# Scores of gathered rows and the chain of maxima moved to earlier hops in the first two layers of a graph attention kernel

## The chip, the cores and the metric

The kernel runs on one core of a Trainium2 chip. The metric is the device time of one execution in microseconds (us). Before the change, three runs gave 7299.5, 7305.31 and 7309.96 us; the median is 7305.31 us.

## The reference, cut to what matters

The input is a graph with 6250 nodes of 256 features and 200,000 edges (`src`, `dst`), ordered by destination. Three graph attention layers run one after the other, the first two with four heads, the third with one; beside them stand a linear attention block and a mixture of eight experts. One attention layer computes:

```python
xh = (h @ W).reshape(n, heads, d)
a_s = (xh * att_src).sum(-1)
a_d = (xh * att_dst).sum(-1)
alpha = leaky_relu(a_s[src] + a_d[dst], 0.2)
amax = segment_max(alpha, dst)
e = exp(alpha - amax[dst])
z = segment_sum(e, dst)
out = segment_sum(xh[src] * (e / z[dst])[:, :, None], dst)
```

Every node has an edge to itself as well. So for each edge a row of its source node is fetched, a score is made, the largest score of the edges with one destination is found, and the rows are summed with the weights `exp(score - largest)`.

## The kernel before, in words

**Tiles.** The edges are cut into rows of 128, and 32 such rows make one round. Each layer has 51 rounds, written out one after the other in `sum_messages`. A gather (line 549) is one indirect DMA that GpSimd issues; it fetches the feature rows of 128 edges. Eight gathers fill one row group `g` of 8 x 128 edges, and a round has four row groups, 0 to 3. The pool of row groups has 8 buffers in the first layer, 9 in the second and 7 in the third (`nrows`).

**Rounds and hops.** A round is written as 16 hops (`for i in range(HSU)`). In hop i of round s, TensorE multiplies the one-hot matrices of two edge rows with their weighted gathered rows (`pair`, line 752), and VectorE adds the product of an earlier pair to the accumulator of the destination block (`add_up`, line 765). After the pairs of hops 3, 7, 11 and 15 a row group is free, and the next gathers into that buffer are issued (`gather`). With 8 buffers, the group that is issued in hop 4j + 3 of round s is group j of round s + 2. With 9 buffers, group j of round s + 2 is issued one freeing earlier, in hop 4j - 1.

**What is made for the next round.** While round s is summed, the weights of round n = s + 1 are made:

- `row_scores` (line 610): ScalarE copies the source scores out of a gathered row group into `asc`, one group at a time. It needs the gather landed. Before the change this is in hops 2, 4, 5 and 7.
- `spread` (line 603): TensorE brings the destination scores to the edges, in hops 0 to 8; VectorE sums three parts of them into `exs` in hop 11 (line 796).
- `scores` (lines 587 and 591): in every second round, TensorE makes the destination scores of two rounds in hops 1 to 4, and ScalarE copies them out in hop 5.
- `maxima`: a chain of ten links that finds the largest score of each destination. Link 0 is a TensorE transpose of `asc` (line 621); link 1 two VectorE scans and two products (625 to 630); link 2 TensorE (633); link 3 VectorE (637 to 646); link 4 TensorE and one VectorE product (649, 652); link 5 VectorE (655 to 670); link 6 TensorE (674 to 677); link 7 VectorE (681 to 694); link 8 the exponentials on ScalarE (696, 697); link 9 VectorE writes the weights and factors (701, 705).
- `weigh_step` (lines 715 and 722): VectorE and ScalarE multiply gathered rows with the weights, about two hops ahead of the pair that reads them.

A link is either early in its hop (ahead of `weigh_step`, `add_up` and `pair`) or late (behind the pair, ahead of `spread`). Before the change:

| Link | 0 | 1 | 2 | 3 | 4 | 5 | 6 | 7 | 8 | 9 |
|---|---|---|---|---|---|---|---|---|---|---|
| Works on | PE | DVE | PE | DVE | PE, DVE | DVE | PE | DVE | ACT | DVE |
| Hop | 7 late | 8 late | 9 early | 10 early | 10 late | 11 late | 12 early | 13 early | 14 early | 14 late |

**What sets the order.** `Order.keep` pins each engine to the order of the text. An engine whose next instruction waits holds up all that is written behind it on that engine. Pieces of other work (linear attention in the first layer, the finished blocks of every layer, the experts in the third) are dealt out at the end of hops by `beside`. SyncE issues the loads of tables and lanes in text order too; GpSimd issues gathers only. The chain and `scores` share one PSUM bank, `sm`, of which there is one.

Of the kernel before, what the change touches and what calls it, by code (L numbers as in the profile page):

```python
# [7 lines left out]
F32 = mybir.dt.float32  # L8
# [7 lines left out]
P = 128  # L16
# [7 lines left out]
SU = 32  # L24
# [430 lines left out]
def leaky(nc, out, x):  # L455
    nc.vector.scalar_tensor_tensor(out, x, SLOPE, x, op0=OP.mult, op1=OP.max)
# [26 lines left out]
def sum_messages(tc, pools, consts, q, node_rows, adn, h, acc, beside, begin, slot, last,  # L483
# [9 lines left out]
    nc = tc.nc  # L493
    lp, tb, gp, hp, tp, wk, pmp, smp = pools
# [46 lines left out]
    def gather(m):  # L541

        if m >= end * subs:
            return
        s, k = divmod(m, subs)
        t = rows[m] = gp.tile([P, SUB, W], F32, name="g")
        for c in range(SUB):
            i = k * SUB + c
            nc.gpsimd.indirect_dma_start(  # L549
                out=t[:, c, :], out_offset=None, in_=node_rows,  # L550
                in_offset=bass.IndirectOffsetOnAxis(ap=T[s]["src"][:, i:i + 1], axis=0))

    def load_lanes(m):

        if m >= end * subs:
            return
        t = lanes[m] = tp.tile([P, SUB, P], BF16, name="hot_t")
        load(tc, t, bass.AP(tensor=q["lane_rows"].tensor,
                            offset=q["lane_rows"].offset + m * SUB * P,
                            ap=[[0, P], [P, SUB], [1, P]]))  # L560

    def compare_lanes(m):
        if m < end * subs:
            nc.vector.tensor_scalar(lanes[m], lanes[m], consts["pidx"], None, op0=OP.is_equal)  # L564

    def hot(m):

        s, k = divmod(m, subs)
        if s >= end:
            return  # L570
        t = M[s].setdefault("hots", {})[k] = hp.tile([P, SUB, P], F32, name="hot")
        nc.vector.tensor_tensor(  # L572
            t, consts["lane_ps"][:, None, :].to_broadcast([P, SUB, P]),
            T[s]["lane"][:, k * SUB:(k + 1) * SUB, None].to_broadcast([P, SUB, P]),
            op=OP.is_equal)
# [5 lines left out]
    def scores(s):  # L581


        pt = bank()[:, :3 * hs].rearrange("p (k c) -> p k c", k=3 * h)
        for i in range(4):
            for k in range(i * 3 * h // 4, (i + 1) * 3 * h // 4):
                nc.tensor.matmul(pt[:, k, :], adt[:, k // 3, k % 3, :], T[s]["block_hot"],
                                 start=True, stop=True)
            yield
        A[s] = wk.tile([P, h, 3, SU], BF16, name="adc")  # L590
        nc.scalar.copy(A[s].rearrange("p k j c -> p (k j) c"), pt)
# [5 lines left out]
    def spread(s, c0, n):  # L597

        m = M[s]
        if c0 == 0:  # L600
            m["ex"] = smp.tile([P, SU, h, 3], F32, name="ex")
        for c in range(c0, c0 + n):
            nc.tensor.matmul(m["ex"][:, c], lanes[s * subs + c // SUB][:, c % SUB, :],  # L603
                             adc(s)[:, :, :, c // 2], start=True, stop=True)

    def row_scores(s, k):
        m = M[s]
        if k == 0:
            m["asc"] = wk.tile([P, h, SU], F32, name="asc")
        nc.scalar.copy(m["asc"][:, :, k * SUB:(k + 1) * SUB].rearrange("p h c -> p c h"),  # L610
                       rows[s * subs + k][:, :, body:])

    def maxima(s):

        m, t = M[s], T[s]
        asc = m["asc"]
# [34 lines left out]
        on = lp.tile([HEADS, HEADS], F32, name="on")  # L651
        nc.vector.tensor_scalar(on[:h, :h], consts["ident"][:h, :h], run, None, op0=OP.mult)
        yield
        u = lp.tile([P, 2, h, SU], F32, name="u")
        nc.vector.tensor_add(u[:, 0], asc, m["exs"])
        pick = lp.tile([P, 2, SU], F32, name="pick")
        nc.vector.tensor_tensor(pick[:hs], pc[:hs],
                                cmask[:, None, :].to_broadcast([hs, 2, SU]), op=OP.mult)
# [19 lines left out]
        mt = m["mt"] = sm[:, k:k + hs].rearrange("p (h c) -> p h c", h=h)  # L678
        yield

        nc.vector.tensor_tensor(u[:, 1], mt, m["exs"], op=OP.add)
        leaky(nc, u, u)
        w = m["w"] = wk.tile([P, h, SU], F32, name="w")
# [19 lines left out]
        for k in range(subs):  # L703
            i = slice(k * SUB, (k + 1) * SUB)
# [19 lines left out]
    def weigh_step(s, i):  # L724

        c = (i // 2 + 1) * GRP
        s, c = s + c // SU, c % SU
        if not 0 <= s < end:
            return
        if half:  # L730
            weigh(s, c + half + i % 2, 1, nc.scalar)
            if i % 2:
                weigh(s, c, half, nc.vector)
        else:
            weigh(s, c + i % 2 * 2, 2, nc.scalar)

    def blocks(s, k):
        if s >= end:
            return
        loads, M[s].setdefault("blocks", {})[k] = nc.values_load_multi_w_load_instructions(  # L740
            T[s]["block"][0:1, k * GRP:(k + 1) * GRP], engines=(mybir.EngineType.DVE,),
            min_val=0, max_val=NB - 1,
            skip_runtime_bounds_check_because="blocks are counted from 0 to NB - 1")

    sums = []

    def pair(s, i):
        m = M[s]
        t, k = rows[s * subs + 2 * i // SUB], 2 * i % SUB
        pm = pmp.tile([P, W], F32, name="pm")  # L750
        for j in range(2):
            nc.tensor.matmul(pm, m["hots"][2 * i // SUB][:, k + j, :], t[:, k + j, :],  # L752
                             start=(j == 0), stop=(j == 1))
        sums.append((s, i, pm))

    def add_up(ahead=1):
        while len(sums) > ahead:
            s, i, pm = sums.pop(0)
            b = bass.ds(M[s]["blocks"][i // GRP][i % GRP], 1)
            if i == 0:  # L760
                at = acc[:, b, :body].rearrange("p b (h d) -> p (b h) d", h=h)
                nc.vector.tensor_tensor(at, at, M[s]["fac"][:, :, None].to_broadcast([P, h, d1]),
                                        op=OP.mult)
            at = acc[:, b].rearrange("p b w -> p (b w)")
            nc.vector.tensor_tensor(at, at, pm, op=OP.add)  # L765
# [16 lines left out]
    for s in range(-1, end):  # L782
        n = s + 1
        made = n < end
        if made:
            M[n] = M.get(n, {})
        ahead = iter(())
        if n % 2 and n + 1 < end:
            ahead = scores(n + 1)
        for i in range(HSU):  # L790

            if made and i in (2, 4, 5, 7):
                row_scores(n, (2, 4, 5, 7).index(i))
            if made and i == 11:
                M[n]["exs"] = wk.tile([P, h, SU], F32, name="exs")
                nc.vector.tensor_reduce(M[n]["exs"].rearrange("p k c -> p c k"), M[n]["ex"],
                                        axis=AX.X, op=OP.add)
            if made and i in (9, 10, 12, 13, 14):
                next(chain)
            if s < 0 and i * GRP < NB:  # L800
                nc.vector.memset(acc[:, i * GRP:min(NB, (i + 1) * GRP), :], 0.0)

            weigh_step(s, i)
            add_up()
            if s >= 0:
                pair(s, i)
                if i % GRP == GRP - 1:
                    gather(s * subs + i // GRP + nrows)
            if i % GRP == 1 and (i > 1 or s >= 0):
                hot((n if i > 1 else s) * subs + (i // GRP - 1) % subs)  # L810
            if i % GRP == 2:
                k = i // GRP + 1
                blocks(s + k // subs, k % subs) if s >= 0 or k == subs else None
            if made and i == 7:
                chain = maxima(n)
            if made and i in (7, 8, 10, 11, 14):
                next(chain, None)

            if made and i < 9:
                spread(n, 4 * i - max(0, i - 5), 4 - i // 5)  # L820
                if i in (1, 3, 6, 8):
                    load_lanes(n * subs + (1, 3, 6, 8).index(i) + nlanes)
                if i in (1, 3, 5):
                    compare_lanes(n * subs + i // 2 + 1)
            if made and i == HSU - 1:
                compare_lanes((n + 1) * subs)
            if 1 <= i <= 5:
                next(ahead, None)
            if i == 8 and s + 3 not in T:
                tables(s + 3)  # L830
            if s >= 0:
                if s * HSU + i in slots:
                    slot(slots.index(s * HSU + i), lay)
                if i == HSU // 2 and s == end - 1:
                    last(lay)
                beside.step()
            order.keep()
        for x in (T, M):
            x.pop(s - 1, None)
# [520 lines left out]
class Experts:  # L1360
# [17 lines left out]
    def next(self):  # L1378
        while len(self.ready) < 3 and self.todo:
            self.more()  # L1380
        return self.ready[0]
# [302 lines left out]
```

## Time and profile before

| What | Value |
|---|---|
| Median of three runs | 7305.31 us |
| Profiled execution, its own time | 8248.33 us |
| Span in the profile (first to last instruction) | 8246.6 us |
| Mean granted TensorE clock | 0.797 |
| TensorE busy | 5848.3 us, 71% |
| VectorE busy | 4702.2 us, 57% |
| ScalarE busy | 3408.8 us, 41% |
| GpSimd busy | 4819.9 us, 58% |
| Gathers (line 549) | 4896, mean 979 ns |
| Transposes of `asc` (line 621) | 153, from 219.6 to 8080.6 us |

The profiled execution is 943 us longer than the median of the runs, so its parts cannot be taken over one to one. PE stands for TensorE, DVE for VectorE, ACT for ScalarE, POOL for GpSimd. A wait is written as: engine, tile and line that waited, an arrow, who ended the wait, and then the sum in us, the number of waits, and the longest. "Issue" means that the profile shows nothing it waited for, and "remote" that the semaphore that ended the wait could not be put down to an instruction. Ends of matmuls are modelled in this profile. The summing of the first layer lies between 271 and 2774 us, that of the second between 2906 and 5304, that of the third between 5409 and 8154.

### The profile page before, as it was taken

The page shows a single profiled execution, that of the slowest core. Times are in us where ns is not written, and L with a number is a line of the kernel's source. Part 1 is how long each engine was busy: PE and PEld are TensorE (multiplying, and loading weights), DVE is VectorE, ACT ScalarE, POOL GpSimd, SP SyncE. Part 2 cuts the span into 40 slices and gives each one's busy share as a digit, 9 for nine tenths or more (in the row PEclk, how much of TensorE's full clock was granted, in tenths as well). Part 3 has the DMA queues.
Part 4 walks back from the last instruction along what each step waited for, and adds up shares of the span by engine and source line. Part 5 has one row for each costly group of instructions (what it writes and reads, how often), then busy time and mean ns, then how long its engine had stood idle before and what let it go on. Part 6 is the DMA issues. An engine that isn't in the chain of part 4 may idle for free. (4 is left out here: it accounts for less than half of the span.)

```text
span 8246.6 us, 97731 instructions
## 1 busy us (share of the span) xinstructions
PE 5848.3 (71%) x24601; PEld 4071.4 (49%) x24601; DVE 4702.2 (57%) x13248; ACT 3408.8 (41%) x10628; POOL 4819.9 (58%) x4942
## 2 busy tenths in 40 slices
PE   4577777766666356555665666548888998988998
PEld 3355555544444244344444444336566666665666
DVE  4456676667765365555555665544555555555553
ACT  2345454444434234333333343324444444444443
POOL 2566566666666456666666666465555555655651
PEclk8787778776766677766667776769999999999999
DMA  5444444444444334444444444344555554554553
GB/s 162 118 128 130 118 134 123 127 126 135 140 125 121 94 109 130 120 123 122 122 124 130 124 125 129 94 113 143 143 146 144 149 146 143 157 144 135 151 148 96
DMA packets 616288, 1070.05 MB, mean 130 GB/s; under 512 B 193175, under 2 KB 348167, under 8 KB 615706
## 3 DMA queue, kind: packets, MB, share of 16 engines
q0 software_dynamic: 236672, 661.50, 29.1%
q1 hardware_dynamic: 370590, 389.03, 15.8%
q10 hardware_dynamic: 8444, 13.02, 0.4%
q8 instruction: 212, 3.47, 0.2%
q14 instruction: 370, 3.03, 0.1%
HBM read 1008.69 MB, written 56.03 MB: 129 GB/s over the span
## 5 line engine op out<-in xcount | busy, mean ns | idle before, releaser
L549 POOL DMA_INDIRECT g<-node_rows,src_t x4896 | 4791.2, 979 | 3165.2 <-issue 1332.1
L752 PE MATMUL pm<-g,hot 128*128 128x264 f32 (+1 forms) x9792 | 3345.2, 481 | 855.2 <-issue 392.4
L752 PEld LDWEIGHTS pm<-g,hot 128*128 128x128 f32 x9792 | 2156.1, 235 | 1542.6 <-issue 632.2
L722 ACT ACTIVATE g<-g,w 128x65 f32<-128x65 f32 (+1 forms) x8160 | 2378.0, 369 | 207.0 <-issue 203.0
L765 DVE TENSOR_TENSOR acc<-acc,pm 128x264 f32 (+1 forms) x2448 | 1030.6, 421 | 844.6 <-remote 327.1
L572 DVE TENSOR_TENSOR hot<-lane_ps,lane_t 128x1024 f32<-128x1024 f32 x612 | 743.6, 1215 | 0.0
L715 DVE TENSOR_TENSOR g<-g,lane_ps 128x520 f32<-128x520 f32 x816 | 558.9, 685 | 34.7 <-issue 31.7
L603 PEld LDWEIGHTS <-hot_t 128*128 128x128 bf16 x4896 | 357.1, 105 | 372.6 <-issue 171.0
L696 ACT ACTIVATE w<-w 128x128 f32<-128x128 f32 (+1 forms) x153 | 43.1, 282 | 1011.6 <-DVE w L684 686.9
L603 PE MATMUL ex<-adc,hot_t 128*128 128x12 bf16 (+1 forms) x4896 | 360.4, 179 | 87.5 <-issue 72.3
L1607 PE MATMUL fa<-moe_w,moe_h 128*128 128x256 f32 x1600 | 398.7, 392 | 30.4 <-DVE eo L1612 12.6
L1595 PE MATMUL fa<-et,moe_w 128*128 128x512 f32 (+1 forms) x832 | 396.1, 600 | 29.8 <-DVE eo L1612 13.2
L1595 PE MATMUL fk<-et,moe_w 128*128 128x512 f32 (+1 forms) x832 | 387.2, 588 | 11.9 <-DVE eo L1588 5.1
L1600 ACT ACTIVATE moe_h<-fa,moe_b 128x512 f32<-128x512 f32 (+1 forms) x208 | 137.6, 662 | 597.6 <-PE fa L1595 425.0
L1607 PE MATMUL fk<-moe_w,moe_h 128*128 128x256 f32 x1536 | 377.0, 389 | 8.0 <-DVE eo L1612 6.9
L610 ACT COPY asc<-g 128x32 f32<-128x32 f32 (+1 forms) x612 | 136.5, 223 | 528.9 <-DMA g<-node_rows,src_t 464.6
L1612 DVE SCALAR_TENSOR_TENSOR eo<-fa,share,eo 128x256 f32<-128x256 f32 x200 | 96.1, 480 | 432.7 <-PE fa L1607 212.2
L1607 PEld LDWEIGHTS fa<-moe_w,moe_h 128*128 128x128 f32 x1600 | 297.9, 193 | 83.0 <-ACT moe_h L1600 18.2
L564 DVE TENSOR_SCALAR hot_t<-hot_t,pidx 128x1024 bf16<-128x1024 bf16 x612 | 304.3, 497 | 42.5 <-DMA hot_t<-q_lane_rows 34.0
L1607 PEld LDWEIGHTS fk<-moe_w,moe_h 128*128 128x128 f32 x1536 | 288.5, 192 | 49.8 <-DVE eo L1612 9.3
L649 PE MATMUL sm<-cf,hrow 4*128 4x64 f32 (+1 forms) x306 | 71.4, 320 | 331.3 <-DVE cf L646 144.9
L639 DVE TENSOR_TENSOR_SCAN rf<-joins_t,rf,sm 4x32 f32<-4x32 bf16 (+1 forms) x153 | 41.2, 269 | 371.4 <-remote 279.3
(385 smaller groups left out, 5781.9 us busy)
## 6 DMA issues: line engine op xcount, KB each, us to landing
hot_t<-q_lane_rows SPq DMA_DIRECT2D x612, 256.0 KB
moe_w<-in_L_ffn_W_dram SPq DMA_DIRECT2D x208, 512.0 KB
g<-node_rows,src_t POOLq DMA_INDIRECT x4896
ea<-node_rows SPq DMA_DIRECT2D x24, 528.0 KB
et<-xnt SPq DMA_DIRECT2D x24, 512.0 KB
hid<-eo SPq DMA_DIRECT2D x24, 512.0 KB
eold<-hid SPq DMA_DIRECT2D x24, 512.0 KB
node_rows<-r ACTq DMA_DIRECT2D x12, 528.0 KB
```

The source lines that it names most:

```text
L549: nc.gpsimd.indirect_dma_start(out=t[:, c, :], out_offset=None, in_=node_rows, in_offset=bass.IndirectOffsetOnAxis(ap=T[s]["src"][:, i:i + ...
L564: nc.vector.tensor_scalar(lanes[m], lanes[m], consts["pidx"], None, op0=OP.is_equal)
L572: nc.vector.tensor_tensor(t, consts["lane_ps"][:, None, :].to_broadcast([P, SUB, P]), T[s]["lane"][:, k * SUB:(k + 1) * SUB, None].to_broa ...
L603: nc.tensor.matmul(m["ex"][:, c], lanes[s * subs + c // SUB][:, c % SUB, :], adc(s)[:, :, :, c // 2], start=True, stop=True)
L610: nc.scalar.copy(m["asc"][:, :, k * SUB:(k + 1) * SUB].rearrange("p h c -> p c h"), rows[s * subs + k][:, :, body:])
L715: nc.vector.tensor_tensor(x, x, w[:, :, c:c + n].rearrange("p h c -> p c h")[:, :, :, None].to_broadcast([P, n, h, d1]), op=OP.mult)
L722: nc.scalar.activation(x, x, AF.Copy, scale=w[:, j, c + i:c + i + 1])
L752: nc.tensor.matmul(pm, m["hots"][2 * i // SUB][:, k + j, :], t[:, k + j, :], start=(j == 0), stop=(j == 1))
L765: nc.vector.tensor_tensor(at, at, pm, op=OP.add)
L1595: nc.tensor.matmul(pt[:, :w], w1[:, k, j * P:(j + 1) * P], xt[:, k, :w], start=(k == 0), stop=(k == 1))
L1600: nc.scalar.activation(hx[:, j, :w], pt[:, :w], AF.Gelu, bias=self.b1[:, e * 4 + j:e * 4 + j + 1])
L1607: nc.tensor.matmul(pt[:, :C], hx[:, j, t * P:(t + 1) * P], w2[:, j, :], start=(j == 0), stop=(j == 3))
```

## The change

In the first two layers the row scores are taken in hops 1, 2, 3 and 5 (first layer) or 1, 2, 3 and 4 (second layer). `scores` runs from hop 0 on. The chain starts late in hop 5 and has one link in each hop up to 12, all late; links 8 and 9 stay in hop 14:

| Link | 0 | 1 | 2 | 3 | 4 | 5 | 6 | 7 | 8 | 9 |
|---|---|---|---|---|---|---|---|---|---|---|
| Hop, layers 1 and 2 | 5 late | 6 late | 7 late | 8 late | 9 late | 10 late | 11 late | 12 late | 14 early | 14 late |

The sum `asc + exs` (line 655) needs `exs`, which is made in hop 11; it moves from link 5 to link 7, in all three layers. The third layer, with 7 buffers, keeps the hops of before.

```diff
@@ maxima
-        u = lp.tile([P, 2, h, SU], F32, name="u")
-        nc.vector.tensor_add(u[:, 0], asc, m["exs"])
         pick = lp.tile([P, 2, SU], F32, name="pick")
...
+        u = lp.tile([P, 2, h, SU], F32, name="u")
+        nc.vector.tensor_add(u[:, 0], asc, m["exs"])
         nc.vector.tensor_tensor(u[:, 1], mt, m["exs"], op=OP.add)
@@ sum_messages
+    if gp.bufs > 7:
+        taken, early = (1, 2, 3, 5 if gp.bufs == 8 else 4), 0
+        hops = (14,), (5, 6, 7, 8, 9, 10, 11, 12, 14)
+    else:
+        taken, early = (2, 4, 5, 7), 1
+        hops = (9, 10, 12, 13, 14), (7, 8, 10, 11, 14)
...
-            if made and i in (2, 4, 5, 7):
-                row_scores(n, (2, 4, 5, 7).index(i))
+            if made and i in taken:
+                row_scores(n, taken.index(i))
...
-            if made and i in (9, 10, 12, 13, 14):
+            if made and i in hops[0]:
                 next(chain)
...
-            if made and i == 7:
+            if made and i == hops[1][0]:
                 chain = maxima(n)
-            if made and i in (7, 8, 10, 11, 14):
+            if made and i in hops[1]:
                 next(chain, None)
...
-            if 1 <= i <= 5:
+            if 0 <= i - early <= 4:
                 next(ahead, None)
```

## The prediction

> **What bounds the kernel now.** I read the busy time per layer first, then the spacing of the rounds, then the waits of the first two layers, then single rounds in the timeline. The busy times (engines in the order PE, PE weight load, DVE, ACT, POOL, then the granted clock, the DMA share and GB/s):
>
> ```profile
> core 0: us, PE busy (x) PEld busy (x) DVE busy (x) ACT busy (x) POOL busy (x), PEclk, DMA share, GB/s
> 271.00:2774.00 2503.00, 1768.80 (x7326) 1214.22 (x7325) 1639.74 (x4523) 1151.35 (x4092) 1533.28 (x1568) 0.76 0.44 126
> 2906.00:5304.00 2398.00, 1452.14 (x5943) 1025.14 (x5941) 1413.58 (x3776) 943.11 (x3691) 1524.86 (x1560) 0.71 0.44 122
> 5409.00:8154.00 2745.00, 2420.23 (x10358) 1683.62 (x10357) 1435.07 (x4269) 1214.20 (x2590) 1549.66 (x1576) 0.93 0.49 142
> ```
>
> The third layer is filled by PE (88%). In the first two no engine passes 71%. The layers take 2503 / 51 = 49.1 and 2398 / 51 = 47.0 us a round. What holds them is waiting between engines. GpSimd has the hardest floor below: a gather is 0.95 us and the 0.30 us of "issue" behind it, so 32 gathers are 40 us a round.
>
> The waits of the first layer, then (from the sixth line) of the second:
>
> ```profile
> POOL g L549 <- issue: 404.5, 1319, 2.0
> PE sm L633 <- DVE ends L630: 49.8, 21, 5.1
> PE sm L674 <- DVE mx_f L662: 49.0, 21, 5.7
> PE sm L649 <- DVE cf L646: 40.4, 8, 14.2
> ACT asc L610 <- DMA g<-node_rows,src_t: 36.1, 9, 10.0
> ...
> DVE rf L639 <- remote: 178.0, 22, 11.8
> PE sm L649 <- DVE cf L646: 100.5, 14, 10.6
> PE sm L674 <- DVE mx_f L662: 75.5, 32, 11.1
> PE sm L633 <- DVE mx_b L626: 56.0, 13, 7.9
> PE sm L633 <- DVE ends L630: 43.1, 9, 7.3
> ```
>
> The reader is to see that TensorE stands still at the three small matmuls of the chain. All waits of these lines on PE, smaller rows included, are 80 us (L633), 61 (L649) and 65 (L674) in the first layer, and 145, 197 and 87 in the second. One round of the first layer shows how (start, duration, engine, line; idle time before it in brackets):
>
> ```profile
> 2205.94 0.23 DVE L630 TENSOR_SCALAR ends<-cmask,mx_b 128x32 f32<-128x32 f32 x1
> 2206.23 0.37 PE L633 MATMUL sm<-ends,hcol 128*4 128x64 f32 x2 [0.73 <-DVE ends L629]
> ...
> 2215.27 0.48 DVE L662 TENSOR_TENSOR_SCAN mx_f<-cut_t,carry,sm 128x128 f32<-128x128 bf16 x1
> 2215.81 0.59 PE L674 MATMUL sm<-on,ones 4*128 4x4 f32 x2 [2.72 <-DVE mx_f L662]
> 2217.55 3.73 PE L752 MATMUL pm<-g,hot 128*128 128x264 f32 x8
> ```
>
> L633 is written right behind the VectorE link that feeds it (8 late, 9 early), and so is L674 (11 late, 12 early). No pair stands between, so PE waits for the whole VectorE link, and the next pairs queue behind. L649 has one pair between.
>
> Part of the waits is of another kind:
>
> ```profile
> 3450.67 0.27 PE L633 MATMUL sm<-ends,hcol 128*4 128x64 f32 x2 [3.73 <-issue]
> ...
> 3462.30 0.27 DVE L639 TENSOR_TENSOR_SCAN rf<-joins_t,rf,sm 4x32 f32<-4x32 bf16 x1 [9.54 <-remote]
> ```
>
> The matmul that L639 needs is drawn as over at 3450.9, yet VectorE goes on 11.4 us later. Perfetto Trace Analysis in the Trainium skill (Summary: the profiler window per engine type) says that a matmul's end in a trace is an estimate. The row agrees, and I cannot say whether such late ends are in the unprofiled runs, which are 943 us shorter. So I give L649's waits less weight.
>
> **The change part by part.**
>
> *Nothing is added or removed.* The same instructions run, the DMAs too; only places in the order differ. `asc + exs` (0.27 us) moves from link 5 to link 7: it leaves PE's path to L674 and enters the path to the exponential, 1.5 hops before that is due. Nothing in sum. In the third layer it moves 0.19 us the same way; PE covers it there.
>
> *Links 2 and 6 get a hop of cover.* Every PE link now stands a full hop behind the VectorE link that feeds it, with a pair, an addition and a weighing between. VectorE links cost 1.0 to 2.2 us; a hop is 49.1 / 16 = 3.1 us. So the waits at L633 and L674 should mostly go: 80 + 65 = 145 us in the first layer, 145 + 87 = 232 in the second. An engine that stands less is soon held by something else (VectorE is busy 66% and 59%), so I count 60%: 87 and 139 us. If no other wait took over, it is all of it; if VectorE sets the pace in these hops, nothing. Of L649, which goes from half a hop to a full one, I count a quarter: 15 and 49 us. Sum 102 and 188 us.
>
> *Row scores earlier.* What is late next is the gather of group 3. In the first layer it is issued in hop 15 and read in hop 5, no longer 7: 6 hops instead of 8. Eight gathers are 10.0 us, and asc copies that a DMA ended began at the median 1.97 us behind the end of the eighth gather. Taking that landing for every round, and the end of PE's pair in hop 5 from the timeline, PE's transpose finds the scores in time by 4.5 us at the median, and is late in about an eighth of the rounds, 20 us in all. ScalarE is there earlier: going back by the eight weighings of two hops, its waits for group 3 grow from 29 to 90 us and for group 2 from 0 to 14. Behind it are weighings that PE needs two hops on; I count a third of those 75 us. Cost 20 + 25 = 45 us. In the second layer (nine buffers) the distance goes from 12 hops to 9; PE has 14.6 us to spare in hop 5, ScalarE loses 6 us. Nothing.
>
> *`scores` one hop earlier.* Its matmuls wait for the last reads of the bank `sm` (L705, late in hop 14): two hops, no longer three; the pair of hop 0 waits for the same writes already. The copy is in hop 4, the transpose into the bank in hop 5. Nothing; without cover it would be one 0.24 us matmul group every second round. SyncE's loads and GpSimd's gathers keep their places.
>
> *The clock.* TensorE: Matmul & The Clock Gate in the Trainium skill (What's actually happening) has the clock at half after an idle window of some 3.4 us and full after a busy one. The rows show 0.76 and 0.71 against 0.93 in the dense third layer. By the rule this could go against the change: work spread evenly at 60 to 70% fills fewer windows than dense bursts. At 0.65 in both layers, PE's work would grow by 1769 x (0.76/0.65 - 1) + 1452 x (0.71/0.65 - 1) = 433 us, at most half of it exposed. The other way, 0.76 in the second layer would take off 1452 x (1 - 0.71/0.76) = 96. The waits removed are mostly 2 to 3 us, shorter than that window, so I take the rows and no change of clock.
>
> *Sum.* In the profiled execution: 102 - 45 + 188 = 245 us of 8248. For the unprofiled runs I put a cap on it. Spreading the 943 us evenly over 153 rounds takes off 6.2 us each: 42.9 and 40.8 us a round. The gather floor of 40 us then leaves 51 x 2.9 = 148 us in the first layer and 51 x 0.8 = 41 in the second. Scaled by 7305 / 8248 = 0.886 the first layer's 57 is 50 us, below its cap. The second's 188 is 167, far above; but an even spread is only my guess, as the late ends are more frequent there and gathers may be cheaper unprofiled. Between 41 and 167 I take 60, near the floor's end. So 50 + 60 = 110 us: 7305 - 110 = **7195 us**.
>
> **The rivals.**
>
> *Gathers set the pace.* The second layer is at the gather floor already in unprofiled runs, only the first gains: 7305 - 50 = 7255. For: 40 of 47 us. Against: in the second layer `asc` hardly waits for a landing in the profile, so gathers are not late there.
>
> *The stalls are real and all go.* 0.886 x 245 = 217, perhaps with a little clock: 7085.
>
> *Slower: group 3 comes too late.* The place is L610 in hop 5 of the first layer, with L621 behind it on PE. If unprofiled hops are shorter by 6.2 / 16 = 0.39 us while the gathers are not, six hops lose 2.3 of the 4.5 us to spare. It decides once the mean stall passes 110 / 51 = 2.2 us a round. At 4 us on both engines it is 51 x 4 - 110 = 94 us slower: 7400. For: 18 of 50 rounds have ScalarE late even by the profiled pace. Against: PE's median slack. A half clock by the rule above would end on the same side.
>
> *It does nothing.* The same waits show up one hop later, since VectorE is late anyway: 7305.
>
> **How the numbers follow.** Forecast 0.40; gathers set the pace 0.15; all stalls go 0.12; late group 3 0.28; nothing 0.05. A difference below 0.2% (15 us) cannot be told from none here. Faster: 0.40 x 0.95 + 0.15 x 0.8 + 0.12 = 0.62. Slower: 0.28 + 0.02 = 0.30. Same: the remaining 0.08. The range must reach into both: from 7070, just past the full gain, to 7370, which leaves out about half of the slower case (0.14). The forecast's own range is 7130 to 7260.
>
> **What would show each step.** Right: waits of PE at L633 and L674 in the first two layers fall by half or more, rounds shorten to about 47 and 44 us in the profile, and waits of L610 for the gather in the first layer grow to about 100 us, in the second not. Wrong: those waits move to L639, L657 or L681 on DVE with rounds as long as before; or L621 waits for L610 over 2 us a round in the first layer; or the third layer changes.

## The result, and the profile after

Seven runs of the changed kernel gave 7320.23 to 7337.85 us, median 7331.19 us; seven of the kernel before, measured beside them, 7293.84 to 7310.5 us, median 7301.99 us. The ratio is 1.0038, with a 95% interval of 1.0027 to 1.005: the change makes the kernel 0.4% slower. The forecast was 7195 us.

To read the numbers one thing has to be known: the kernel before takes 7302 to 7309 us (medians) on some chips and 8244 to 8353 us on others. The profile of before that the prediction reads, with 8248 us and a granted clock of 0.797, is like those of the second kind; the runs compared above, and the profile after, are of the first. Profiling costs little: a new profile of the unchanged kernel (label e0 below) took 7318.45 us, and the runs of that kernel beside it 7291.76 to 7321.9 us. So the 943 us between profile and runs were not what profiling costs. The new profile is the one to set beside that of after: span 7316.6 us, granted clock 0.844, against 7333.0 us and 0.844 after (own time 7334.85 us). The spans are 16.4 us apart, the medians above 29 us: e0 is a single execution, 10 us above the median of its runs, so a few us between two single profiles say little.

In the changed kernel the line numbers of the prediction's chain have shifted: the pair is L760 (L752 before), the addition L773 (L765), link 5 ends with L660 and L667/L668 (L662, L669/L670), link 6 is L672, L673, L675 (L674, L675, L677). L591 to L649 are where they were.

Busy time per layer after (the same columns as in the prediction: length of the stretch, PE, weight load, DVE, ACT, POOL, then clock, DMA share, GB/s), each from the first copy of scores to the last addition:

```profile
core 0: us, PE busy (x) PEld busy (x) DVE busy (x) ACT busy (x) POOL busy (x), PEclk, DMA share, GB/s
178.00:2371.00 2193.00, 1630.26 (x7364) 1111.30 (x7363) 1648.54 (x4576) 1156.49 (x4119) 1585.55 (x1623) 0.82 0.53 148
2405.00:4521.00 2116.00, 1298.80 (x5986) 892.27 (x5986) 1414.12 (x3832) 934.02 (x3728) 1585.25 (x1621) 0.77 0.52 143
4557.00:7241.00 2684.00, 2389.31 (x10389) 1670.96 (x10390) 1453.37 (x4315) 1223.38 (x2607) 1586.57 (x1620) 0.93 0.51 148
```

The same view of e0, the kernel before:

```profile
178.00:2354.00 2176.00, 1622.62 (x7362) 1124.28 (x7361) 1653.28 (x4576) 1156.63 (x4120) 1590.05 (x1623) 0.82 0.54 149
2389.00:4511.00 2122.00, 1294.69 (x5986) 901.95 (x5986) 1421.48 (x3830) 935.42 (x3727) 1594.39 (x1620) 0.77 0.52 143
4547.00:7224.00 2677.00, 2386.87 (x10388) 1669.89 (x10389) 1455.82 (x4315) 1223.25 (x2608) 1587.33 (x1620) 0.93 0.52 148
```

Over whole layers the busy times and the clocks nearly agree; the lengths differ: +17 us in the first layer, -6 in the second, +7 in the third. In the second the gathers themselves happened to take 9 us less (1594.39 to 1585.25 us of GpSimd). The third layer's first 50 rounds take 2583 us in one profile of the new order (e14) and 2604 us in another (e12), with nothing edited in that layer between them, so the 7 us are not read. The rounds of the first two layers last 42.6 and 41.1 us after (42.2 and 41.3 before), beside the 41 us that 32 gathers take (0.98 us in the mean and 0.30 to the next).

Waits in the first layer, after (engine, tile and line, what ended the wait; then us in total, times, longest):

```profile
ACT asc L610 <- DMA g<-node_rows,src_t: 363.6, 73, 10.1
DVE mx_f L625 <- PE sm L621: 194.9, 37, 26.8
PE sm L621 <- ACT asc L610: 187.8, 36, 27.6
...
DVE rf L639 <- PE sm L633: 29.7, 18, 2.9
...
PE sm L672 <- DVE mx_f L660: 3.6, 1, 3.6
...
PE sm L649 <- DVE cf L646: 2.3, 1, 2.3
...
PE sm L633 <- DVE ends L630: 1.0, 1, 1.0
```

and of e0:

```profile
ACT asc L610 <- DMA g<-node_rows,src_t: 327.1, 62, 11.5
...
PE sm L621 <- ACT asc L610: 162.7, 27, 27.4
DVE mx_f L625 <- PE sm L621: 153.0, 24, 24.4
...
PE sm L674 <- DVE mx_f L662: 42.7, 22, 3.4
...
PE sm L633 <- DVE ends L630: 24.6, 17, 2.4
PE sm L649 <- DVE cf L646: 15.8, 15, 2.5
```

The cover did what the prediction wanted of it: TensorE's waits at L633, L649 and link 6 together, smaller rows included, fall from 105 to 15.5 us, and in the second layer from 77.5 to 18.7. Part of them went over to VectorE: it now waits at L639 for the matmul of L633, 29.7 us in the first layer (10.6 before) and 60.5 in the second (0.6 before), one of the signs that the prediction named for being wrong. And two readings that the prediction had not are in these rows. First, on such a chip the three matmuls had only 105 and 77.5 us of waits to give, where its profile showed 206 and 429. Second, the largest wait by far is that of ScalarE for a gather, and the chain stands behind it. The second layer shows this most plainly, after:

```profile
ACT asc L610 <- DMA g<-node_rows,src_t: 878.1, 123, 12.7
DVE mx_f L625 <- PE sm L621: 487.2, 48, 19.9
POOL g L549 <- issue: 437.3, 1435, 0.3
PE sm L621 <- ACT adc L591: 212.6, 25, 10.2
PE sm L621 <- ACT asc L610: 171.6, 26, 20.7
...
DVE rf L639 <- PE sm L633: 60.5, 37, 3.0
...
PE sm L672 <- DVE mx_f L660: 3.6, 1, 3.6
```

and of e0:

```profile
ACT asc L610 <- DMA g<-node_rows,src_t: 836.0, 129, 12.7
DVE mx_f L625 <- PE sm L621: 539.7, 49, 18.3
POOL g L549 <- issue: 432.1, 1418, 0.3
PE sm L621 <- ACT asc L610: 354.7, 51, 21.2
...
PE sm L674 <- DVE mx_f L662: 37.1, 32, 3.1
...
DVE rf L639 <- PE sm L633: 0.6, 2, 0.4
```

GpSimd's longest pause ahead of a gather is 0.3 us in both: it issues one gather after the other through the whole layer. TensorE stands at the transpose for 355 us before and 384 after. In every second round it now waits for L591, the copy of the destination scores, as ScalarE stands at L610 ahead of that copy. One round of the second layer after (start, duration, engine, line; idle time before it in brackets):

```profile
3416.64 0.95 POOL L549 DMA_INDIRECT g<-node_rows,src_t  x1 [0.30 <-issue]
3417.01 0.24 ACT L610 COPY asc<-g 128x32 f32<-128x32 f32 x1 [6.83 <-DMA g<-node_rows,src_t]
3417.30 0.33 PE L621 MATMUL sm<-ident,asc 128*128 128x128 f32 x1 [3.46 <-ACT asc L610]
```

ScalarE waits 6.8 us for the gather and TensorE 3.5 us behind it, with the gathers back to back meanwhile. Waits that are taken out of the chain in such a round come back here.

**GpSimd's idle time** is the measure of what there was to gain. Adding up, from the timeline, what a gather's pause exceeds 0.31 us (the first twelve row groups, which fill the empty buffers, left out): 55.9 us in the first layer of e0 and 0.0 in its second; 76.1 and 0.0 after. And nearly all of it lies in one stretch, the rounds 10 to 28 of the first layer. There the second part of linear attention is dealt out beside the rounds: in e0 its matmuls run from 564.5 us (L1160, in round 8) to 1445.9 us (L1211, in round 28). The finished blocks' work is dealt out after it, and its first addition (L1431) comes at 1461.6 us, also in round 28. By where the rounds begin:

| First layer, us (idle of GpSimd in brackets) | rounds 0-9 | 10-28 | 29-49 |
|---|---|---|---|
| e0, before | 417.0 (0.0) | 837.7 (55.8) | 857.1 (0.0) |
| after | 419.6 (4.7) | 846.5 (71.3) | 863.5 (0.2) |

In the other profiles with gathers whole, on chips of the same kind, the rounds 10 to 28 take 831.6 and 837.2 us with the old order (e1, e13), 845.9 to 849.4 us with the new one in this layer (e2, e12, e14), and 838.6 to 843.1 us with the orders in between (e3 to e5). The end of the layer's last gather moves by 15.9 us (2318.3 to 2334.2): 20 us more of idle time, less 4 us that the gathers themselves took less in that execution. Another 2.6 us lie between that end and the start of the last round (18.4, then 21.0). The 6.4 us of the rounds 29 to 49 are in the main a delay that shows late: counted from the layer's first gather, the last gather of round 28 ends 13.5 us later than before, and the layer's last 16.5.

TensorE's waits within the rounds 10 to 28, after:

```profile
PE pm L760 <- DVE acc L773: 65.5, 48, 3.4
...
PE sm L621 <- ACT asc L610: 14.6, 7, 5.1
```

and of e0:

```profile
PE pm L752 <- DVE acc L765: 40.7, 35, 2.0
...
PE sm L633 <- DVE ends L630: 17.0, 10, 2.4
PE sm L674 <- DVE mx_f L662: 15.5, 9, 3.1
...
PE sm L649 <- DVE cf L646: 9.8, 9, 2.3
PE sm L675 <- DVE new L670: 5.7, 9, 0.7
```

The 48 us at links 2, 4 and 6 are gone, but the pairs wait 25 us more for VectorE's additions, and the transpose 15 us for the scores. Adding up all of TensorE's time from the first pair of round 10 to that of round 29 shows where the loss stands (`sm` holds the chain and `scores`):

| First layer, rounds 10-28 | length, us | TensorE waits | of that at `sm` | at pairs for additions | TensorE busy | granted clock |
|---|---|---|---|---|---|---|
| old order (e0, e1, e13) | 831.6-837.7 | 156.7-159.7 | 47-52 | 43-47 | 670.8-679.7 | 0.844-0.859 |
| new order (after, e2, e12, e14) | 845.9-849.4 | 156.0-158.6 | 15-16 | 70-71 | 686.6-692.3 | 0.834-0.841 |

TensorE waits as long as before, only elsewhere, so the cover wins nothing there. What grows is the busy time of the same matmuls, at a slightly lower clock. Scaling e0's 679.7 us by the clock gives 2.9 us for after (0.8443 to 0.8407) and 8.8 us for e12 (0.8335), an estimate, of the 6.9 and 12.6 us that their busy time is longer; the rest is not explained.

### The profile page after: what moved, and what is told of

The parts are those of the page before. It is cut to its first block, busy times and chain, and to the rows that moved or that the text cites. A ratio compares the mean times of both kernels' runs of the same rounds, so it can differ in the third digit from the quotient of the medians.

```text
span 7333.0 us, 97806 instructions
## 1 busy us (share of the span) xinstructions
PE 5499.8 (75%) x24601; PEld 3804.4 (52%) x24601; DVE 4667.3 (64%) x13248; ACT 3390.0 (46%) x10628; POOL 4818.9 (66%) x4942
## 5 line engine op out<-in xcount | busy, mean ns | idle before, releaser
L760 PE MATMUL pm<-g,hot 128*128 128x264 f32 (+1 forms) x9792 | 3115.8, 452 | 774.4 <-DVE acc L773 347.1
L760 PEld LDWEIGHTS pm<-g,hot 128*128 128x128 f32 x9792 | 1985.1, 218 | 1423.6 <-DVE acc L773 459.2
L722 ACT ACTIVATE g<-g,w 128x65 f32<-128x65 f32 (+1 forms) x8160 | 2351.7, 369 | 0.1
L773 DVE TENSOR_TENSOR acc<-acc,pm 128x264 f32 (+1 forms) x2448 | 1026.8, 419 | 230.1 <-PE pm L760 170.9
L610 ACT COPY asc<-g 128x32 f32<-128x32 f32 (+1 forms) x612 | 138.0, 226 | 1744.2 <-DMA g<-node_rows,src_t 1743.8
L621 PE MATMUL sm<-ident,asc 128*128 128x128 f32 (+1 forms) x153 | 61.5, 402 | 760.5 <-ACT asc L610 547.1
L625 DVE TENSOR_TENSOR_SCAN mx_f<-cut_t,sm 128x128 f32<-128x128 bf16 (+1 forms) x153 | 63.5, 415 | 889.6 <-PE sm L621 889.3
L621 PEld LDWEIGHTS sm<-ident,asc 128*128 128x128 f32 (+1 forms) x153 | 22.7, 149 | 833.4 <-ACT asc L610 604.8
```

Source lines behind the costliest of these rows:

```text
L722: nc.scalar.activation(x, x, AF.Copy, scale=w[:, j, c + i:c + i + 1])
```

## The experiments

**The kernel before once more.** Nothing edited.

> The kernel before, unchanged, profiled once more, since the changed kernel's profile shows none of the late matmul ends and has a span (7333.0 us) like its unprofiled runs. Theory A (the first two layers run at the pace of the gathers already, and the changed order only moves the wait for them to a worse place): the span is close to 7300 us, a round takes about 42 us in the first layer and 40.5 us in the second, GpSimd's gathers with their issue gaps fill over 90% of both, and ScalarE waits for landings at L610 for some 500 us or more over the two layers. Theory B (the loss is the late group 3 of the first layer alone): the first layer is some 30 us shorter than in the changed kernel (2222 us between first and last), the second layer is equal or longer. If the stalls of the first profile are real: span 8200 us again, rounds of 49 and 47 us.

Measured: 7318.45 us in its profiled execution, span 7316.6 us; the runs of before beside it have a median of 7308.51 us. It is the profile used above.

**One layer at a time.**

```diff
-    if gp.bufs > 7:
+    if gp.bufs == 9:     # e1: the second layer only
+    if gp.bufs == 8:     # e2: the first layer only
```

> Only the second layer (9 buffers) has the new hops, the first keeps those of before. Theory A: the second layer carries the larger part of the loss, since in the changed kernel PE stands at L621 for some 384 us there, so 7320 to 7335 us (ratio 1.002 to 1.005). Theory B: no loss, 7290 to 7305 us (ratio 0.998 to 1.001).

> Only the first layer (8 buffers) has the new hops, the second keeps those of before. Theory A: 7295 to 7315 us (ratio 0.999 to 1.002). Theory B: the whole loss, 7325 to 7340 us (ratio 1.003 to 1.005).

Measured: the second layer alone 7304.69 us, ratio 1.0001 (0.9991 to 1.0011); the first alone 7330.63 us, 1.0037 (1.0024 to 1.005). The whole loss is the first layer's. In the second the new order is worth nothing either way, though TensorE's waits at the chain fell by 59 us there in the profile after. The addition of L655 stays moved in all layers in both, and in e3 to e5, so e1 shows that this move costs nothing.

**A chain one hop later.** In both layers the scores are taken in hops 2, 4, 5, 6 and the chain starts late in hop 6, with all the cover of the change.

```diff
-        taken, early = (1, 2, 3, 5 if gp.bufs == 8 else 4), 0
-        hops = (14,), (5, 6, 7, 8, 9, 10, 11, 12, 14)
+        taken, early = (2, 4, 5, 6), 0
+        hops = (14,), (6, 7, 8, 9, 10, 11, 12, 13, 14)
```

> Both layers: row scores in hops 2, 4, 5 and 6, the chain late in each hop from 6 to 13, exponentials early in 14. Each link has a full hop of cover as in the changed kernel, and the gathers have one hop more in the first layer and two more in the second. Theory A: the engines stand at L621 for less, and the cover of the links stays: faster than the changed kernel, near the time before or a little under it, 7260 to 7310 us (ratio 0.994 to 1.001). Theory B: the first layer has one hop more, most of the loss goes, 7300 to 7315 us. If the even spacing of the links itself costs time: about as the changed kernel, 7325 to 7335 us.

Measured: 7318.22 us, 1.0014 (1.0007 to 1.0021). GpSimd's idle time in the first layer is 62.9 us. A later read and chain cost less: the loss is about 10 us, not the 22 of e2. The clock is lower here, 0.835 to 0.84 in the runs against 0.842 to 0.848 before; in the rounds 10 to 28 TensorE waits 8 us less than in e0 (148.9 us) and is busy 9 us longer (688.7 us, at 0.838).

**The early scores alone, and the latest place for the chain.** In e4 only the first layer's scores move (hops 1, 2, 3, 5), and the chain keeps its old hops. In e5 the first layer's chain starts late in hop 8, one hop later than before the change, and the scores are in hops 2, 4, 6, 8.

```diff
-    if gp.bufs > 7:
-        taken, early = (1, 2, 3, 5 if gp.bufs == 8 else 4), 0
-        hops = (14,), (5, 6, 7, 8, 9, 10, 11, 12, 14)
+    if gp.bufs == 8:
+        taken, early = (1, 2, 3, 5), 1                        # e4
+        hops = (9, 10, 12, 13, 14), (7, 8, 10, 11, 14)        # e4
+        taken, early = (2, 4, 6, 8), 1                        # e5
+        hops = (10, 11, 12, 13, 14), (8, 9, 10, 11, 14)       # e5
```

> First layer only: the row scores in hops 1, 2, 3 and 5, all else as before (scores in 1 to 5, the chain from hop 7 with its old places). If ScalarE's early standing at L610 by itself delays weighings and so the freeing of row groups: the loss of the first-layer change comes back in part, GpSimd's idle time in the first layer rises from 56 us towards 76, 7315 to 7330 us (ratio 1.001 to 1.003). If the standing of PE at L621 in hop 5 is what delays the pairs and so the next gathers: no loss, 7300 to 7312 us (ratio 0.999 to 1.001).

> First layer only, the other way: row scores in hops 2, 4, 6 and 8, the chain from 8 late (links at 8 late, 9 late, 10 early, 10 late, 11 early, 11 late, 12, 13 and 14 early, 14 late), less cover than before. If the round follows from GpSimd's idle time, which follows from how late the pairs behind the wait for group 3 are: idle time falls below 56 us by some 5 to 15, 7290 to 7303 us (ratio 0.998 to 0.999). If cover of the links decides: slower than before, 7320 to 7360 us.

Measured: e4 7314.88 us, 1.0009 (1.0002 to 1.0016), with 64.5 us of idle time; e5 7312.82 us, 1.0008 (1.0001 to 1.0016), with 56.3. So the early scores alone cost about 6 us (interval 1.5 to 12), a smaller part of the loss, and the earlier chain, together with `scores` one hop earlier, the rest. By row groups, the idle time ahead of the gathers of groups 0, 1, 2 and 3 is 15.5, 8.9, 10.7 and 20.8 us in e0, 19.5, 15.2, 12.8 and 28.6 after, and 15.6, 10.0, 11.4 and 27.5 in e4: group 3's loss is there with the early scores alone, and that of groups 0 and 1 comes only with the earlier chain. Moving the chain the other way gains nothing, where 5 to 15 us less idle time was one expectation: no place tried brings the idle time below that of before.

**A quarter of the gathers taken out.** Of eight gathers of a row group two are left out, and one plain load of fixed rows from SyncE fills their places, so GpSimd needs about 30 us a round (the sums are then wrong). If the gathers set the pace, the change must show its gain here.

```diff
+        load(tc, t[:, 3::4, :], node_rows[0:2 * P, :].rearrange("(n p) c -> p n c", p=P))
         for c in range(SUB):
+            if c % 4 == 3:
+                continue
```

> The order of before, with two of the eight gathers of each row group replaced by one plain load of 256 fixed rows that SyncE issues, so that GpSimd needs 30 us a round and no longer 40; the edges of these two rows are summed with the wrong source rows. If gathers set the pace of the first two layers: these fall from 42.2 and 41.3 us a round to 34 to 39, and the kernel to 6700 to 7050 us. If not: within 1% of 7305 us.

> The changed order with the same replacement of two gathers in eight. If the gather pace hid a gain from the cover of the links: faster than the order of before with thin gathers by 40 to 150 us. If the waits at L633 and L674 cost nothing even without that pace: within 15 us of it. If the earlier row scores cost in themselves: slower than it.

Measured: the order of before 6485.97 us (ratio to before 0.8881, 0.8869 to 0.8892), that of after 6462.97 us (0.885, 0.8839 to 0.8862). The sign turns round: 23 us faster. Where the gathers bind and where they don't is read from the rounds, here in us:

| Layer, rounds | e0 | after | e6, thin, before | e7, thin, after |
|---|---|---|---|---|
| first, 0-9 | 417.0 | 419.6 | 372.4 | 347.9 |
| first, 10-28 | 837.7 | 846.5 | 833.6 | 834.0 |
| first, 29-49 | 857.1 | 863.5 | 756.5 | 750.5 |
| second, 0-49 | 2062.5 | 2054.5 | 1555.3 | 1561.7 |

A quarter fewer gathers shorten the second layer by a quarter: there the gathers set the pace, and at 31 us a round they still do. In the first layer they set it in the rounds 0 to 9 and 29 to 49. Once relieved, rounds 0 to 9 gain 24.5 us from the change, a gain of the kind that was forecast; rounds 29 to 49, just as relieved, gain only 6 us. In the rounds 10 to 28 the relief is worth 4 us of 838, and the change nothing. That stretch has another limit; its busy times in e6 (columns as above):

```profile
590.00:1380.00 790.00, 644.04 (x2918) 441.00 (x2917) 635.17 (x1736) 452.59 (x1480) 424.31 (x432) 0.85 0.52 147
```

TensorE is busy 82% and VectorE 80% of it, GpSimd 54%. With all gathers, in e0:

```profile
642.00:1480.00 838.00, 679.96 (x3071) 466.27 (x3072) 672.06 (x1837) 478.03 (x1569) 597.07 (x608) 0.84 0.53 146
```

Here they are busy 81% and 80%, and GpSimd 71%, against 75% in the second layer (1594.39 of 2122 us).

**Eight row groups in the second layer.** If the ninth buffer were what keeps the second layer from losing, the order of after would lose there with eight.

```diff
-            lp, gp, wk = pool("lay", 1), pool("rows", (8, 9, 7)[l]), pool("scores", 2)
+            lp, gp, wk = pool("lay", 1), pool("rows", (8, 8, 7)[l]), pool("scores", 2)
```

> The order of before, with 8 row group buffers in the second layer too (8, 8, 7). If the count of buffers is what makes the freeing of groups matter: GpSimd, which never idles there with 9, idles for 5 to 60 us in the second layer, 7310 to 7365 us. If it is the first layer's other work (linear attention) that makes pairs late: GpSimd still does not idle there, 7300 to 7315 us.

> The changed order with 8 buffers in the second layer too, group 3 read in hop 5 there as in the first. If the count of buffers decides: the second layer now loses as the first does, some 15 to 30 us more than the changed kernel, and more idle time of GpSimd in the second layer than in the order of before with 8 buffers. If the other work of the first layer decides: within 10 us of the changed kernel, 7325 to 7340 us.

These two fell on a chip where the kernel before takes 8347.84 us. Measured: before's order 8347.59 us (1.0003, 0.9982 to 1.0023), after's 8292.44 us (0.9918, 0.9887 to 0.9949): on that chip the new order is faster. Waits of the second layer in e8:

```profile
DVE rf L639 <- remote: 184.0, 18, 14.2
...
PE sm L649 <- DVE cf L646: 171.5, 17, 14.5
ACT asc L610 <- DMA g<-node_rows,src_t: 127.1, 17, 12.2
...
PE sm L633 <- DVE ends L630: 93.6, 18, 8.2
```

and in e9:

```profile
ACT asc L610 <- DMA g<-node_rows,src_t: 265.2, 47, 13.6
DVE rf L639 <- remote: 112.4, 21, 18.5
...
PE sm L633 <- DVE ends L630: 56.0, 10, 8.4
```

Here the rows are those of the prediction's profile: TensorE waits at the chain, VectorE for a semaphore that can't be put down to an instruction, and the gather is, in e8, a lesser wait. The rounds of the first two layers last 50.3 and 48.8 us in e8, GpSimd is idle for 388 us in the second, so there is room, and the new order takes 52 us off its first 50 rounds (2437.6 to 2385.8 us). The first layer gains nothing even here, though GpSimd is idle for 469 us in it: 2515.7 us in e8, 2514.1 in e9. The question on buffers was put again on a chip with before at 7307.86 us, with the change itself beside it:

> The changed kernel itself, unchanged. Where the kernel before takes about 7300 us: 7325 to 7340 us, as measured, with no idle time of GpSimd in the second layer. Where the kernel before takes about 8300 us, with late matmul ends: if those leave the gathers enough time, the cover of the links shows, mostly in the second layer, 30 to 150 us faster than the kernel before.

> The order of before with 8 row group buffers in the second layer too. Where the kernel before takes 7300 us: if the count of buffers decides whether GpSimd idles, 5 to 60 us of idle time in the second layer and 7310 to 7365 us; if the other work of the first layer does, none and 7300 to 7315 us. Where it takes 8300 us: within 0.3% of it, as measured.

> The changed order with 8 buffers in the second layer too. Where the kernel before takes 7300 us: if the count of buffers decides, the second layer loses 10 us or more against the order of before with 8 buffers there; if the other work of the first layer does, 7325 to 7340 us, as the changed kernel. Where it takes 8300 us: 0.5 to 1.1% faster than before, as measured.

Measured: the change 7334.55 us, 1.0036 (1.0023 to 1.005), so the result repeats; before with eight 7309.82 us, 1.0002 (0.9994 to 1.0011); after with eight 7328.21 us, 1.0031 (1.0021 to 1.0042). GpSimd's idle time in the second layer is 0.0 us in both with eight groups. So eight buffers do not make the second layer lose, and their number isn't what sets the first layer apart.

**Half of the gathers taken out.** As above, with every second gather replaced.

```diff
-        for c in range(SUB):
+        load(tc, t[:, 1::2, :], node_rows[0:4 * P, :].rearrange("(n p) c -> p n c", p=P))
+        for c in range(0, SUB, 2):
```

> The order of before, four of the eight gathers of each row group replaced by one plain load of 512 fixed rows from SyncE, so that GpSimd needs 20 us a round; the edges of these four rows are summed with the wrong source rows. With two of eight replaced, the second layer still ran at 31.1 us a round against 30 us of gathers. If gathers set the pace alone: the second layer falls to 27 us or less, the first to 38 to 39, the kernel to 6200 to 6350 us. If something else holds the second layer at 31: 6430 to 6490 us.

> The changed order with the same replacement of four gathers in eight. If the cover of the links is worth its stalls once gathers are out of the way: the first layer is shorter than in the order of before by 25 to 60 us and the second by 15 to 60, 40 to 120 us in all. If the second layer has no such gain at all: only the first layer's 20 to 35 us.

On the chip of e8: before's order 6405.15 us (0.7677 of before there), after's 6348.42 us (0.7608), 57 us or 0.9% faster, about 24 us in each of the first two layers. The 6405 us fit neither expectation (6200 to 6350, or 6430 to 6490). The second layer's rounds take 30.3 us, hardly less than the 31.1 of e6 on the other kind of chip, with GpSimd idle for 469 us, so at half of the gathers something else holds it. The rounds 10 to 28 of the first take 827.7 and 832.8 us, and the change brings nothing there a second time. These two lengths are not to be set beside e0's as they stand, for with all gathers that chip takes 991.8 us for these rounds (e8). Half of the gathers took away the late ends too: of the 260.7 us that VectorE waits for "remote" at L639 in e8, none is left in e10 and e11.

**Linear attention taken out.** It is left out, and its input copied in its place; the finished blocks' work then begins in round 2 and no longer in round 28. If linear attention's work is what the new order collides with, the loss of the first layer should go.

```diff
+    for t0, n in groups():
+        x = wk.tile([P, GRP, C + 2 * HEADS], F32, name="ea")[:, :, :C]
+        Where(tc, t0, n).load(x, i["x"])
+        yield
+        Where(tc, t0, n).store(res, x)
+        yield
+    return
     wqkv = i["L0_mix_Wqkv_t"].rearrange("(k p) o -> p k o", p=P)
```

> The order of before without the linear attention: in its place the same generator only copies x to its result, so that the output lacks it. If the other work of the first layer makes the pairs behind the wait late and so GpSimd idle: idle time falls from 56 us to under 10, the first layer runs at the gathers' pace as the second does, 41 to 41.5 us a round and no longer 42.2, and the kernel gains 30 to 60 us and what the start and end of the layer save. If the idle time has another cause: it stays near 56 us.

> The changed order with the linear attention left out in the same way. If the other work decides: no loss is left, within 10 us of the order of before without it, no idle time of GpSimd in the first layer. If the loss belongs to the early row scores with 8 buffers whatever else runs: still 15 to 30 us slower.

> The changed order without the linear attention once more (its place taken by a copy of x). Where the kernel before takes about 7300 us: if the other work of the first layer is what makes GpSimd idle there, the idle time in the first layer falls from 76 us to under 10 and a round takes 41 to 41.5 us; if the early scores with 8 buffers idle it whatever else runs, 60 us or more stay and a round takes 42 us or more. Where it takes about 8300 us: 1 to 2.2% faster than before, as measured, and the question stays open.

All three fell on chips where the kernel before takes 8243.58 us (e15, e16) or 8353.03 us (e17), so they can't say why the first layer loses on the others. Measured: before's order 8203.39 us (0.9944, 0.9923 to 0.9964), after's 8104.04 us (0.9817, 0.9782 to 0.9852) and, on the other chip, 8178.66 us (0.9795, 0.9763 to 0.9827). But set beside e8 and e9 they answer the question for chips of their own kind:

| First layer's first 50 rounds, us (rounds 10-28 in brackets) | old order | new order |
|---|---|---|
| with linear attention (e8, e9) | 2515.7 (991.8) | 2514.1 (992.7) |
| without (e15; e16 and e17) | 2448.1 (934.9) | 2397.6 (912.3) and 2400.4 (916.4) |

With it the cover wins nothing in the first layer, without it 50 us, as in the second (2403.0 to 2350.3 us in e15 and e16). The whole kernel says the same: 55 us faster from e8 to e9, 99 from e15 to e16. So there the work of linear attention takes the gain away, directly or by pushing the finished blocks into the rounds from 28 on.

## Why the prediction was wrong

*Cover for links 2, 4 and 6: right.* It forecast that the waits at L633 and L674 fall by half or more; those of L633 and link 6 fell from 87 to 13 us in the first layer and from 71 to 16 in the second.

*What the waits were worth, second layer: wrong, in the step "Spreading the 943 us evenly over 153 rounds … 148 us in the first layer and 41 in the second".* The room had to be read from how long GpSimd is idle, and that is 56 us and 0 us on the chips that were timed. The floor of 40 us was too low as well: it takes 0.95 us for a gather, where the mean in its own profile is 0.979 us, which makes 41 us a round and, by the same even spread, leaves the second layer nothing. The text called the even spread a guess, and then took "60, near the floor's end" for the second layer, above the 41 of its own sum. Measured, the second layer's part is 0 (e1: ratio 1.0001, 0.9991 to 1.0011). There the rival "gathers set the pace" was right. What was held against it, that `asc` hardly waits for a landing, came from a profile of the other kind of chip: the wait is 836 us in e0.

*The first layer's 57, scaled to 50: wrong in sign, in the step "so I count 60%".* It did not split the layer. In its rounds 0 to 9 and 29 to 49 the gathers bind already, so cover can bring nothing; e7 shows that it brings 24.5 us in rounds 0 to 9 when they don't, and 6 in rounds 29 to 49. In the rounds 10 to 28, where GpSimd has its 56 us of idle time, the share that counts is none: TensorE's waits there are 157 to 160 us with the old order and 156 to 159 with the new, as what leaves the chain comes back at the pairs that wait for VectorE's additions. That is the clause "if VectorE sets the pace in these hops, nothing", and the rival "it does nothing", which was given a chance of 0.05. Beyond nothing, these rounds get 9 us longer, and that is TensorE's busy time. e4 shows the early scores at fault for a smaller part of the loss, and e3 and e5 that a later chain loses less.

*"Row scores earlier. … Cost 20 + 25 = 45 us": the side right, the place wrong.* ScalarE's waits for the gather in the first layer, forecast to grow "to about 100 us", were 327 us already and are 364 after. But most of that growth, and most of the standing at L621, lies in gather-paced rounds, where it costs nothing. Of TensorE's 188 us at L621 in the first layer, 15 fall in the rounds 10 to 28. The rival "group 3 comes too late" was right that the kernel gets slower, in the first layer, with group 3 the one that loses most. Its mechanism, with 4 us a round and 94 us in all, is not what the runs show: the early scores alone cost 6 us, and TensorE's standing behind them in the rounds 10 to 28 is those 15 us in all. So that the kernel got slower, as that rival said, is in part luck.

*In the second layer "ScalarE loses 6 us. Nothing": the total right, the reason wrong.* There was no time to spare; ScalarE waited 836 us before and 878 after. It costs nothing as the gathers pace the layer. Nor was the copy of the destination scores free of effect: 213 us of TensorE's wait at L621 are now put down to it, hidden in the same way.

*The clock: right for the layers, not for the rounds that lose.* The granted clock is 0.82 and 0.77 in the first two layers with both orders. By the rule of the Trainium skill that it weighed (TensorE: Matmul & The Clock Gate, What's actually happening) work spread evenly could have lost clock or won it. In the rounds 10 to 28 of the first layer the new order has 0.834 to 0.841 where the old one has 0.844 to 0.859, worth some 3 to 9 us by the estimate above, a term that was put at nothing.

*The late ends.* The prediction could not say whether a matmul drawn as over 11.4 us ahead of its reader was only a matter of how ends are drawn, and gave L649's waits less weight. They go with real time: they are in the profiles of the chips whose timed runs are 13 to 14% longer (L639 waits up to 19.4 us for "remote" in e8), and in the first layer of e0 the longest wait at L639 is 2.1 us. On such a chip they are gone when half of the gathers are (e10, e11). That they are the cause of the longer time wasn't tested.

*What stays open.* Why TensorE's matmuls take longer in the rounds 10 to 28 with the new order: the lower clock makes a part of it by the estimate, and what lowers the clock was not tested. That linear attention is what leaves no room there is shown for chips of the slower kind (e8, e9, e15 to e17), by single profiles on different chips; for the others it is argued from the place. The change with its own nine buffers was not measured on a chip of the slower kind.

## What to carry to other kernels

Before costing a stall, ask which engine never pauses in that stretch, and cut a layer where its other work begins and ends: here 59 of 77 us of waits on TensorE went and were worth nothing, since the gathers went out back to back beside them. An engine's pauses beyond its usual gap, added up between its first and its last instruction, bound what a reordering can win there; the stalls of another engine do not. Add up all waits of the engine, not only those that were aimed at: 32 us less at the chain were 28 us more at the pairs. When the profiled time and the timed runs stand 13% apart, profile the unchanged kernel once more before subtracting anything.

## What was not expected of the hardware

The same kernel takes 7302 to 7309 us on some chips and 8244 to 8353 us on others. On the latter the mean granted clock is about 0.79 (0.793 in e8, 0.797 in the first profile) against 0.844, and VectorE waits at L639 for up to 19.4 us (e8) for what the profile can't put down to an instruction. With half of the gathers gone there is no such wait at that place, at a clock of 0.891 (e10). The order of a kernel is worth different things on the two: with eight row groups in the second layer the new order is 0.3% slower on one kind (7309.82 to 7328.21 us) and 0.7% faster on the other (8347.59 to 8292.44 us).

A gather costs GpSimd 0.98 us in the mean and 0.30 us to the next, and nothing tried here shortened that: the second layer's rounds keep at that floor, with 41.1 us for 32 gathers and 31.1 for 24.

The order of the instructions alone can move the granted clock of the whole kernel: with the chain one hop later (e3) all 17 runs have 0.835 to 0.84, and the runs of before beside them 0.842 to 0.848.
